# State-space layers: one PSUM tag for two rotating decay buffers, or one tag for each buffer

## Chip, cores and metric

The kernel runs on one core of a Trainium2 chip. The metric is the device time of one execution in microseconds (us), as the median of the runs. Beside it there is one execution recorded by the hardware profiler, from which all views of the profile come.

## What is computed

The network has four layers on x of shape 8 x 384 x 32 x 32, each `x = x + layer(group_norm(x))`. Layers 0 and 2 are Mamba state-space layers over 1,024 tokens per sample, with 768 inner channels and 16 states (layer 2 adds a layer norm and an MLP). Layer 1 is a deformable convolution, layer 3 a shift of channels with a small blur. The part that matters here is the recurrence of layers 0 and 2, for each channel d and state n:

```python
def step(h, inp):
    dt_t, B_t, C_t, u_t = inp
    dA = jnp.exp(dt_t[..., None] * A)
    h = dA * h + (dt_t * u_t)[..., None] * B_t[:, None, :]
    y = jnp.einsum('bdn,bn->bd', h, C_t)
    return (h, y)
...
y = jnp.swapaxes(ys, 0, 1) + u * D
y = y * jax.nn.silu(z)
return y @ out_proj_w.T
```

## The kernel before

`Net.ssm_layer` (called for layer 0 and, with the MLP and the shift part, for layer 2) cuts each sample into two halves of 512 tokens. A half is a *step*; there are 16 of them in a layer, and two that belong to one sample are called a pair here (h = 0, then h = 1). A step holds 6 blocks j of 128 channels, and for each block 8 pairs m of states. One (step, j, m) is a *unit*: 48 in a step, 768 in a layer. A unit works on tiles of 128 partitions x 2 states x 512 tokens in fp32:

- `decays` (L434 to L438): ACT computes exp(dt * A) for the two states, one ACTIVATE each, into the tile `da`. This tile lies in PSUM and takes two of the eight banks.
- `inputs` (L440 to L443): POOL computes `db` = dt * u * B in SBUF (three buffers).
- `scan` (L445 to L454): DVE runs the recurrence as one `tensor_tensor_scan` over da and db. It writes h over da in PSUM. For some units ("mine" in the code: m = 0 and 4 in layer 0, m = 0 in layer 2) it writes h to the SBUF tile `hs` instead.
- `keep_last` (L456 to L459): in the steps with h = 0, ACT copies the last state of each row to `st`; the second half starts from it.
- `with_c` (L461 to L467): the product of h and C into `hs`, on DVE (L467), or for the "mine" units on POOL (L464). In layer 2, POOL adds the two states of five of the eight m (`add_pair`, L471).
- `read_out` (L474 to L486): PE sums hs over the states with identity matmuls into the PSUM tile `y` (L484; in layer 0 the D term enters by L480).

When a block's eight units are read out, `close` (L500 to L504) lets DVE multiply y by the gate and write it to u; `out_proj` (L511 to L517) uses u in the next step. The work of the next and previous steps (group norm, input projection `inner`, gate projection `z_proj`, softplus of dt `soft_*`, output projection, MLP) is spread between the units by `plan`. It gives each piece a unit of the step at which it is put behind that unit's own work on ACT, DVE, POOL or PE.

The order of instructions on each engine is thus written out by hand (`manual_schedule`). In the loop over units, iteration i issues in this order: ACT's planned pieces (`run(act[t])`), scan(i), with_c(i) if it is DVE's, keep_last(i), decays(i + 2), DVE's planned pieces, inputs(i + 3), with_c(i) if it is POOL's, POOL's and PE's planned pieces. So decays run two units ahead of their scan, inputs three. Close of block j - 1 is a planned piece of DVE at unit m = 1 of block j.

PSUM's eight banks hold three one-bank tiles of the pool `mm`, two two-bank tiles of the pool `dap`, and `y`. Before the change both tiles of `dap` have one tag, "da", with two buffers. Which of the two buffers a tile gets is decided when the program is built, in the builder's own estimate of which buffer comes free when. In the finished program it is fixed: a tile's first write waits for the last use of the tile that held this buffer before. The same pool serves the shift part (`over_y`, L1706) with 24 tiles.

## Time and profile before

| | us |
|---|---|
| median of 3 runs (9463.35 to 9469.98) | 9464.09 |
| the profiled execution | 9470.15 |
| its span, first to last instruction | 9468.3 |
| layer 0, from the first to the last scan | 63.2 to 3008.5 |
| layer 2, from the first to the last scan | 5953.1 to 9182.3 |
| L438, decays on ACT: 3,072 instructions, mean | 0.691 |
| L453, scan on DVE: 1,536 instructions, into da / into hs, mean | 2.290 / 2.280 |
| L467, C product on DVE: 1,248, mean | 1.225 |
| L464, C product on POOL: 288, mean | 2.355 |
| L443, inputs on POOL: 1,536, mean | 2.354 |

A row of the groups of instructions gives line, engine, operation, tiles, count, busy time, mean duration in ns, and the idle time of the engine just before these instructions with what ended most of it. A row of the list of waits gives who waited for whom, the total in us, how many times, and the longest. A row of a timeline gives start and length in us, engine, line, operation, tiles and count; in brackets is the idle time of that engine ahead of it and what ended it. PEld is TensorE's weight load. A row of the table by windows gives the window, its length, busy time and count of PE, PEld, DVE, ACT and POOL, then the granted TensorE clock, the DMA share and GB/s.

### The profile page before, as it was taken

The numbers are of one execution on the slowest core, as the hardware profiler recorded it, in microseconds if no ns is written. First come the engines' busy times: TensorE is split into PE (matmuls) and PEld (weight loads), VectorE is DVE, ScalarE is ACT, GpSimd is POOL, SyncE is SP. The second block draws the span as 40 slices with busy tenths as digits, with TensorE's granted clock in tenths as the row PEclk, the third lists the DMA queues.
The fourth block names the chain that finished last, engine by engine and source line by source line (L and its number), as shares of the span: only waits on it lengthen the run. The fifth ranks groups of instructions, "written<-read, shape, count | busy, mean of one in ns | idle before, by whom it ended". The sixth has DMA issues, their size and how long they took to land. (4 is left out here: it accounts for less than half of the span.)

```text
span 9468.3 us, 87246 instructions
## 1 busy us (share of the span) xinstructions
PE 8498.2 (90%) x27916; PEld 4527.1 (48%) x27916; DVE 8092.7 (85%) x8857; ACT 6476.0 (68%) x10147; POOL 5825.0 (62%) x3825
## 2 busy tenths in 40 slices
PE   7888888889887999999999997699999999999987
PEld 3333333333333677777777776244343443434333
DVE  7989999999997678778778877899999999999973
ACT  6666666666664678778778777667777777777750
POOL 7989989898897000000000000899999999999974
PEclk8999999999998999999999998799999999999998
DMA  2111211121121333333333333233232433323436
GB/s 94 66 56 46 85 56 49 52 83 56 50 79 40 80 77 89 92 80 88 89 83 87 90 80 87 93 99 96 90 95 88 126 107 96 92 91 90 123 99 127
DMA packets 566064, 791.97 MB, mean 84 GB/s; under 512 B 244243, under 2 KB 397235, under 8 KB 542041
## 3 DMA queue, kind: packets, MB, share of 16 engines
q1 hardware_dynamic: 503492, 775.85, 28.2%
q10 hardware_dynamic: 62100, 10.44, 0.7%
q8 instruction: 223, 3.65, 0.2%
q14 instruction: 249, 2.03, 0.1%
HBM read 716.49 MB, written 69.66 MB: 83 GB/s over the span
## 5 line engine op out<-in xcount | busy, mean ns | idle before, releaser
L443 POOL TENSOR_TENSOR db<-du,bc 128x1024 f32<-128x1024 f32 x1536 | 3607.0, 2354 | 356.3 <-DVE hs L453 184.7
L453 DVE TENSOR_TENSOR_SCAN da<-da,db 128x1024 f32<-128x1024 f32 x1248 | 2857.4, 2290 | 220.5 <-ACT da L438 170.0
L484 PE MATMUL y<-hs,ident 128*128 128x512 f32 x5184 | 2602.9, 639 | 382.2 <-DVE hs L467 229.8
L438 ACT ACTIVATE da<-dt,na 128x512 f32<-128x512 f32 x3072 | 2119.4, 691 | 917.0 <-DVE hs L467 653.8
L411 POOL TENSOR_TENSOR dt<-dt,sp_e 128x512 f32<-128x512 f32 x192 | 243.9, 1270 | 2929.1 <-DVE sp_e L403 2929.1
L484 PEld LDWEIGHTS y<-hs,ident 128*128 128x128 f32 x5184 | 1020.4, 203 | 1860.6 <-issue 1115.9
L1516 PE MATMUL wacc<-fsm,fxk 128*128 128x221 f32 (+34 forms) x10624 | 1667.7, 316 | 91.5 <-DVE fsm L1486 88.8
L1516 PEld LDWEIGHTS wacc<-fsm,fxk 128*128 128x128 f32 x10624 | 1580.6, 196 | 228.4 <-DVE fsm L1486 151.7
L467 DVE TENSOR_TENSOR hs<-da,bc 128x1024 f32<-128x1024 f32 x1248 | 1528.5, 1225 | 91.7 <-DVE da L453 2.3
L1486 DVE TENSOR_TENSOR fsm<-fhy,fhx 128x170 f32<-128x170 f32 (+42 forms) x3216 | 1171.5, 431 | 342.5 <-PE wacc L1516 315.6
L1446 ACT ACTIVATE fhy<-fpyx,cell 128x416 f32<-128x416 f32 (+9 forms) x1280 | 645.6, 576 | 386.8 <-DVE fsm L1486 386.8
L1469 DVE TENSOR_TENSOR fxk<-fxt,fwk 128x1024 f32<-128x1024 f32 (+1 forms) x688 | 788.2, 1182 | 10.8 <-ACT fxt L1248 10.8
L464 POOL TENSOR_TENSOR hs<-hs,bc 128x1024 f32<-128x1024 f32 x288 | 678.3, 2355 | 41.7 <-ACT st L459 41.6
L453 DVE TENSOR_TENSOR_SCAN hs<-da,db 128x1024 f32<-128x1024 f32 x288 | 656.8, 2280 | 49.0 <-POOL db L431 36.1
L471 POOL TENSOR_TENSOR hs<-hs 128x512 f32<-128x512 f32 x480 | 608.9, 1268 | 4.0 <-DVE hs L467 3.5
L567 PE MATMUL ps_m<-hid,wm 128*128 128x512 f32 x1152 | 536.8, 611 | 30.2 <-ACT hid L560 25.3
L545 PE MATMUL ps_h<-t,wm 128*128 128x512 f32 x1152 | 535.9, 603 | 16.5 <-DVE x L574 16.3
L1451 ACT ACTIVATE fhy<-fhy,cols 128x1344 f32<-128x1344 f32 (+10 forms) x368 | 530.8, 1442 | 12.0
L459 ACT COPY st<-da 128x2 f32<-128x2 f32 x624 | 97.8, 157 | 504.3 <-DVE hs L467 503.0
L1157 PE MATMUL ps_off<-fxn,fow 128*98 128x465 f32 (+10 forms) x896 | 386.6, 579 | 0.0
L1433 ACT ACTIVATE fhx<-fpyx,cell 128x544 f32<-128x544 f32 (+8 forms) x640 | 379.9, 666 | 0.0
L567 PEld LDWEIGHTS ps_m<-hid,wm 128*128 128x128 f32 x1152 | 221.6, 195 | 330.8 <-issue 262.4
(203 smaller groups left out, 9865.4 us busy)
## 6 DMA issues: line engine op xcount, KB each, us to landing
bc<-bcd SPq DMA_DIRECT2D x256, 1024.0 KB
fpyx<-fposd SPq DMA_DIRECT2D x640, 256.0 KB
wm<-in_w SPq DMA_DIRECT2D x96, 768.0 KB
x<-x SPq DMA_DIRECT2D x71, 768.0 KB
winr<-in_win SPq DMA_DIRECT2D x192, 192.0 KB
x<-in_x SPq DMA_DIRECT2D x40, 768.0 KB
fpyx<-fposd SPq DMA_DIRECT2D x24, 1024.0 KB
wm<-in_wout SPq DMA_DIRECT2D x48, 384.0 KB
```

The source lines that it names most:

```text
L438: nc.scalar.activation(da[:, i, :], s["dt", j], AF.Exp, scale=na[:, j, n : n + 1])
L443: nc.gpsimd.tensor_tensor(db, du, s["bc"][m][:, 0], ALU.mult)
L453: nc.vector.tensor_tensor_scan(h1, da1, db1, 0.0, ALU.mult, ALU.add)
L464: nc.gpsimd.tensor_tensor(s["hs", m], s["hs", m], c, ALU.mult)
L467: nc.vector.tensor_tensor(hs, s["da", m], c, ALU.mult)
L471: nc.gpsimd.tensor_tensor(hs[:, 0, :], hs[:, 0, :], hs[:, 1, :], ALU.add)
L484: nc.tensor.matmul(s["y"], self.ident, s["hs", m][:, i, :], start=first and i == 0, stop=k == NU - 1 and i == n - 1,)
L567: nc.tensor.matmul(ps, s["w2"][:, f, o * P : (o + 1) * P], s["hid", q][:, f, :], start=(f == 0), stop=(f == 3))
L1446: nc.scalar.activation(hy[:, at : at + (yb - ya) * W], pyx[:, 0, ya * W : yb * W], AF.Abs, bias=bias)
L1469: nc.vector.tensor_tensor(t[:, :n], x, wk[:, j : j + 1, :].to_broadcast([P, n, P]), ALU.mult)
L1486: nc.vector.tensor_tensor(self.sub(sm, at, [(r * w, n), (w, r), (1, w)]), self.sub(hy, hy_at[by] + xa, [(r * W, n), (W, r), (1, w)]), self ...
L1516: nc.tensor.matmul(a[:, ya - 4 * o : yb - 4 * o, xa:xb], k, self.sub(sm, sm_at[by], [(w, yb - ya), (1, w)]), start=False, stop=False,)
```

## The change

The pool gets one buffer per tag, and the tiles get two tags, chosen by the parity of m (units) or of c (chunks of the shift part). As 8 units make a block, parity alternates from unit to unit throughout. The two buffers have the same size and banks as before; a tile of unit k always gets the buffer of unit k - 2.

```diff
@@ ssm_layer
-            dap = ctx.enter_context(tc.tile_pool(name=f"da{li}", bufs=2, space=PSUM))
+            dap = ctx.enter_context(tc.tile_pool(name=f"da{li}", bufs=1, space=PSUM))
@@ decays
-                da = s["da", m] = dap.tile([P, 2, TS], F32, name="da", tag="da")
+                da = s["da", m] = dap.tile([P, 2, TS], F32, name="da", tag=f"da{m % 2}")
@@ over_y (shift part)
-            ps = d["psy", c] = dap.tile([P, 2, TS], F32, name="ps_y", tag="da").rearrange("p a b -> p (a b)")[:, :CH]
+            ps = d["psy", c] = dap.tile([P, 2, TS], F32, name="ps_y", tag=f"da{c % 2}").rearrange("p a b -> p (a b)")[:, :CH]
```

## The prediction

> **What bounds the kernel now.** I read the page first, for the engines' shares and the 40 slices.

> ```profile
> PE 8498.2 (90%) x27916; PEld 4527.1 (48%) x27916; DVE 8092.7 (85%) x8857; ACT 6476.0 (68%) x10147; POOL 5825.0 (62%) x3825
> DVE  7989999999997678778778877899999999999973
> POOL 7989989898897000000000000899999999999974
> ```

> No engine leads by itself. In the two state-space layers (slices 1 to 13 and 26 to 38) DVE and POOL are both near nine tenths. So I then took the busy time of two stretches, one pair of steps (96 units) of layer 0 and one of layer 2.

> ```profile
> 437.80:809.80 372.00, 326.75 (x709) 136.21 (x708) 340.38 (x235) 240.58 (x408) 333.65 (x211) 0.93 0.17 61
> 6776.00:7182.00 406.00, 383.58 (x877) 161.79 (x876) 378.74 (x282) 295.52 (x468) 379.44 (x259) 0.98 0.33 100
> ```

> The columns are length, then PE, PEld, DVE, ACT, POOL busy. DVE is idle 31.6 us of 372 and 27.3 of 406, POOL 38.4 and 26.6. The limit is therefore a chain that passes between DVE, PE and POOL, and what DVE waits for decides. The list of waits has two rows on the decays:

> ```profile
> ACT da L438 <- DVE hs L453: 194.5, 140, 3.1
> DVE da L453 <- ACT da L438: 170.0, 161, 2.2
> ```

> ACT's decays wait for a scan that writes hs (a unit whose C product is POOL's), and then DVE's next scan waits for the decays. One such place, first in ACT's timeline, then in DVE's:

> ```profile
> 520.27 0.15 ACT L459 COPY st<-da 128x2 f32<-128x2 f32 x1
> 521.90 1.42 ACT L438 ACTIVATE da<-dt,na 128x512 f32<-128x512 f32 x2 [1.48 <-DVE hs L453]
> ```

> ```profile
> 518.45 1.23 DVE L467 TENSOR_TENSOR hs<-da,bc 128x1024 f32<-128x1024 f32 x1
> 519.59 2.28 DVE L453 TENSOR_TENSOR_SCAN hs<-da,db 128x1024 f32<-128x1024 f32 x1
> 521.79 0.66 DVE L403 SCALAR_TENSOR_TENSOR sp_e<-sp_w,ps_dt 128x512 f32<-128x512 f32 x1
> 523.41 2.30 DVE L453 TENSOR_TENSOR_SCAN da<-da,db 128x1024 f32<-128x1024 f32 x1 [0.96 <-ACT da L438]
> ```

> The decays of 521.90 are those of the scan of 523.41 (unit k). They could have been written from 520.42 on: the tile of unit k-2 was free when its C product (518.45) ended at 519.68. They wait until 521.87, when the scan of unit k-1 has ended, because in this program their tile lies in the bank pair of unit k-1. DVE then idles 0.96 us.

> [...] gaps of 0.96 us recur here, though the space is there and only the choice of buffer is bad. [...] So decays moved beside a scan should slow neither. The trace agrees: 802 scans with over 1 us of decays beside them take 2.290 us on average, 280 with none 2.282; a decay takes 0.691 us elsewhere and 0.693 at these places, where DVE mostly idles.

> **The change part by part.** (1) *What it moves.* In the built programs every engine has the same instructions in the same order. Before, 110 of 1,560 tiles of the pool lie in the banks of the tile just before (70 in layer 0, 40 in layer 2, none in the shift part); after, none. Only waits differ. At each of the 110 places the decays of unit k lose the wait for scan k-1. The wait moves to the instruction behind them: 94 times to the copy of the last state (L459, which reads that scan's output), 16 times to the decays of k+1.

> (2) *What DVE idles there.* Read scan by scan at those 110: 23 places of 1.54 us (layer 0, m = 5), 47 of 0.96 (layer 0, m = 1; one is 1.31), 40 of 0.96 to 1.62 in layer 2. Sum 127.8 us.

> (3) *How much ACT lets go.* The decays cannot start before ACT's preceding instruction ends. So a place gives the smaller of DVE's gap and ACT's idle time before the decays. At m = 1 in layer 0 ACT idles mostly 1.2 to 1.6, so the whole 0.96 goes. At m = 5 it idles 0.67 (a gate with two table loads is just ahead), so 0.65 of 1.54 goes; 1.27 and 1.24 in the block j = 1. At 14 of the layer 2 places ACT is late by itself: nothing. Sum: layer 0 63.5 us (6.1, 8.5, 8.3, 8.3, 7.9, 8.1, 8.1, 8.2 by pair of steps), layer 2 24.5 (4.36 in the first pair, 2.88 in seven). Together 88.0.

> (4) *What PE takes back.* From 455.7 to 511.8 PE runs out_proj, z_proj, inner and read-outs without a wait:

> ```profile
> 457.53 2.74 PE L517 MATMUL ps_o<-u,wout 128*128 128x512 f32 x6
> ...
> 511.81 0.70 PE L484 MATMUL y<-hs,ident 128*128 128x512 f32 x1 [1.18 <-DVE hs L467]
> ```

> and inside it DVE's close already waits for PE:

> ```profile
> 494.17 0.69 DVE L504 TENSOR_TENSOR u<-y,sz 128x512 f32<-128x512 f32 x1 [0.33 <-PE y L484]
> ```

> Three places lie between (459.39, 474.87, 490.28): what DVE wins there it waits at 494.17. In seven pairs this costs 7 x 0.96 + 8.7 (m = 5) + 5.9 (the third place) = 21.3 us. The first pair has no output projection of an earlier step, so it keeps all. At the other places read closely, y is ready 3.0 to 6.2 us before the close, and PE next waits for DVE (559.6, 588.9, 617.8, 628.5 for the group norm's mean), so its later full stretch starts earlier by as much. Layer 0 keeps 63.5 - 21.3 = 42.2.

> (5) *What POOL takes back.* In the first pair of layer 2 POOL runs without a wait for DVE from 6094 to 6187, and DVE waits 3.34 us for it at 6184.98; the two places in it (0.52 + 0.96) are lost. Elsewhere POOL waits for scans right at the places or soon after, and until it does, db is ready at least 1.8 us before its scan in the cases read: more than one place moves the scan. Layer 2 keeps 23.0.

> (6) *What ACT gives in addition.* After a place ACT is 1.42 us early, DVE 0.96. In layer 2 two short DVE waits that ACT ends follow (6835.01: 0.35; 6901.91: 0.14). I take both in seven pairs: 3.4. Their ends are 0 and 3.4.

> (7) *The new waits.* Behind the copy or the decays of k+1 are queued ACT's further work and POOL's C product (which waits for that copy). The wait ends with scan k-1, and there the old program only began the decays of k; all of it is earlier by up to 1.42 us. Cost 0. From both sides: at worst ACT stands for the scan's 2.28 less the decays' 1.42, 0.86 us, in which it stood idle before too; at best the 1.42 of (6). PE, SP and DMA get no other order: 0.

> Sum: 42.2 + 23.0 + 3.4 = 68.6 us. The profiled execution, 9470.15 (span 9468.3 and 1.9 around it), becomes 9401.5. It is 6.1 over the median of 9464.09; the same saving from there gives 9395.5.

> **The rivals.** *PE takes nothing back* (for: DVE waits at that close are short, 0.33 to 1.32; against: PE has no gap there): 88.0 + 3.4 = 91.4, so 9372.7. *All gaps close* (against: ACT's table loads): 127.8, so 9336.3. *PE takes layer 0 whole*: the full PE stretch of each second step, 628.5 to 705, where DVE waits 3.3, 3.1, 1.0 and 2.1 us for PE, starts by something that does not move. For it: its first weight load also waits for ACT, 4.2 us. Against: the matmul itself starts 2.7 later, on DVE's gn_mv. Then layer 2 alone counts, 26.4: 9437.7. *POOL is the bound* (93% in layer 2; against: it waits for scans right at the places): within 10 us, 9460. *Slower: the granted PE clock falls.* [...] the clock is 0.93 in layer 0, 0.98 in layer 2. PE sets the pace for some 56 + 76 us per pair in layer 0 and about 80 in layer 2 (6898.9 to 6937.7 and a like one), eight times: 1.7 ms. It decides from a fall of 4% there; at 6% it costs 102, net +33: 9497. Against: layer 2 is busier on PE and has the higher clock.

> **How the numbers follow.** Forecast 0.58; PE takes nothing back 0.14; all gaps 0.03; layer 0 lost (wholly, or half with some 48 us left) 0.15; POOL 0.06; slower 0.04. The likeliest time is 9395.5. The range goes from 9372 (nothing taken back) to 9438 (layer 0 lost) and holds 0.87; leaving out either end would leave too much. A difference under 0.2% (19 us) can't be told from none: faster 0.90, same 0.06, slower 0.04.

> **What would show it.** The row of ACT's decays waiting for the scan of hs should fall from 194.5 to near nothing, and DVE's wait for the decays from 170.0 to 60 to 85 (the rest at m = 5 and in layer 2). The scan row's gap at 523.41 should vanish. DVE's wait for PE y at L504 should grow from 33 us by about 20. A pair of layer 0 should take 5.2 us less, a pair of layer 2 3.4. A close that waits no longer than before would show (4) wrong; a pair of layer 0 unchanged, the keeping; scans or decays longer by over 1%, the overlap.

## The result and the profile after

| | before | after | difference |
|---|---|---|---|
| median of the runs, us | 9467.03 (9463.35 to 9472.97) | 9389.55 (9387.00 to 9393.83) | -77.5 |
| ratio, 95% interval | | 0.9919 [0.9907, 0.9931] | |
| profiled execution, us | 9470.15 | 9393.83 | -76.3 |
| up to the first scan of layer 0 | 63.2 | 64.3 | +1.2 |
| layer 0, first to last scan | 2945.4 | 2908.9 | -36.4 |
| between the layers' scans (layer 1) | 2944.6 | 2944.3 | -0.2 |
| layer 2, first to last scan | 3229.1 | 3191.0 | -38.1 |
| after the last scan | 286.1 | 283.4 | -2.7 |

The change is faster by 0.8%, 9 us more than forecast and inside the range. The parts do not fit as well as the sum: layer 0 was to give 42.2 us and gave 36.4, layer 2 was to give 26.4 (steps 5 and 6) and gave 38.1. That these two errors have opposite signs and partly cancel is luck. The stretch after the last scan takes 279.7 to 286.4 us from kernel to kernel, whatever was edited; I do not attribute its 2.7.

The page of the kernel after, the lines of before's first fence:

```profile
PE 8473.1 (90%) x27891; PEld 4507.2 (48%) x27916; DVE 8088.9 (86%) x8857; ACT 6489.3 (69%) x10147; POOL 5825.4 (62%) x3825
...
DVE  7999999999996678778778777899999999999973
...
POOL 7989999999896000000000000899999999999974
```

DVE, ACT and POOL are busy for nearly as long as before, within 0.3% (DVE 8088.9 us against 8092.7, ACT 6489.3 against 6476.0); only idle time went. The same pair of steps in each layer, by windows:

```profile
425.86:792.33 366.47, 325.91 (x712) 135.99 (x711) 340.31 (x236) 241.29 (x409) 333.63 (x211) 0.93 0.18 62
6710.00:7111.55 401.55, 385.06 (x874) 163.08 (x874) 378.48 (x283) 294.90 (x466) 379.62 (x259) 0.97 0.33 101
```

The pair of layer 0 is 5.5 us shorter than before's 372.00, the one of layer 2 4.5 shorter than 406.00 (before's two windows start 10 and 21 us later in their pairs; from first scan to first scan its pairs take 372.04 and 406.19). DVE's and POOL's busy times are those of before. The waits on the decays, and the close's wait for PE:

```profile
ACT da L438 <- DVE hs L453: 74.8, 55, 3.1
...
DVE da L453 <- ACT da L438: 64.1, 69, 2.2
...
DVE u L504 <- PE y L484: 48.0, 21, 3.5
```

DVE's wait for the decays fell from 170.0 to 64.1 us, into the forecast 60 to 85. The close's wait grew from 33.3 to 48.0. ACT's row fell from 194.5 to 74.8 and not to near nothing. I had not split that row: sorted by the scan that ends each wait, 126.4 us of before's were waits for scan k-1 (96 of the 110 places), and 68.1 were units m = 2 and 6 of layer 0, which wait for scan k-2, the owner of their buffer in strict turn too. All 55 waits that remain are of that second kind (47 in layer 0, 8 in layer 2).

The place shown before (scan of 523.41), now in ACT's timeline:

```profile
518.20 0.15 ACT L459 COPY st<-da 128x2 f32<-128x2 f32 x1
518.39 1.42 ACT L438 ACTIVATE da<-dt,na 128x512 f32<-128x512 f32 x2
519.83 0.19 ACT L459 COPY st<-hs 128x2 f32<-128x2 f32 x1
519.93 1.41 ACT L438 ACTIVATE da<-dt,na 128x512 f32<-128x512 f32 x2
```

and in DVE's:

```profile
516.38 1.23 DVE L467 TENSOR_TENSOR hs<-da,bc 128x1024 f32<-128x1024 f32 x1
517.51 2.28 DVE L453 TENSOR_TENSOR_SCAN hs<-da,db 128x1024 f32<-128x1024 f32 x1
519.71 0.66 DVE L403 SCALAR_TENSOR_TENSOR sp_e<-sp_w,ps_dt 128x512 f32<-128x512 f32 x1
520.29 2.29 DVE L453 TENSOR_TENSOR_SCAN da<-da,db 128x1024 f32<-128x1024 f32 x1
```

The decays of 518.39 are written during the scan of 517.51, with no idle time ahead of them. The copy of the last state (519.83) now stands behind them and starts when that scan ends. The scan of 520.29 follows L403 without a gap. It even starts 0.08 us before L403's end (519.71 + 0.66), so a closed place gives 1.04 us, not the 0.96 of the gap.

In what follows, *the ledger* is how much earlier (+) each scan starts than before, unit by unit of a pair (0 to 47 the first step, 48 to 95 the second). It shows where time is won, and where it is given back.

### The profile page after: what moved, and what is told of

Read it like the earlier page. It is cut to its first block, busy times and chain, and to the rows that moved or that the text cites. A ratio compares the mean times of both kernels' runs of the same rounds, so it can differ in the third digit from the quotient of the medians.

```text
span 9392.0 us, 87221 instructions
## 1 busy us (share of the span) xinstructions
PE 8473.1 (90%) x27891; PEld 4507.2 (48%) x27916; DVE 8088.9 (86%) x8857; ACT 6489.3 (69%) x10147; POOL 5825.4 (62%) x3825
## 5 line engine op out<-in xcount | busy, mean ns | idle before, releaser
L453 DVE TENSOR_TENSOR_SCAN da<-da,db 128x1024 f32<-128x1024 f32 x1248 | 2857.4, 2290 | 125.1 <-ACT da L438 64.1
L484 PE MATMUL y<-hs,ident 128*128 128x512 f32 x5184 | 2598.4, 637 | 377.5 <-DVE hs L467 216.9
L438 ACT ACTIVATE da<-dt,na 128x512 f32<-128x512 f32 x3072 | 2120.8, 691 | 812.2 <-DVE hs L467 665.2
L484 PEld LDWEIGHTS y<-hs,ident 128*128 128x128 f32 x5184 | 1013.1, 202 | 1853.0 <-issue 1094.2
L467 DVE TENSOR_TENSOR hs<-da,bc 128x1024 f32<-128x1024 f32 x1248 | 1528.5, 1225 | 91.6 <-DVE da L453 1.4
L453 DVE TENSOR_TENSOR_SCAN hs<-da,db 128x1024 f32<-128x1024 f32 x288 | 656.9, 2281 | 52.0 <-POOL db L431 35.8
L464 POOL TENSOR_TENSOR hs<-hs,bc 128x1024 f32<-128x1024 f32 x288 | 678.7, 2356 | 32.7 <-ACT st L459 32.3
L545 PE MATMUL ps_h<-t,wm 128*128 128x512 f32 x1152 | 538.5, 605 | 16.8 <-DVE x L574 16.6
L567 PE MATMUL ps_m<-hid,wm 128*128 128x512 f32 x1152 | 525.3, 600 | 20.1 <-ACT hid L560 17.2
L459 ACT COPY st<-da 128x2 f32<-128x2 f32 x624 | 98.2, 157 | 512.0 <-DVE hs L467 509.8
L567 PEld LDWEIGHTS ps_m<-hid,wm 128*128 128x128 f32 x1152 | 217.3, 192 | 314.8 <-issue 252.5
```

Source lines behind the costliest of these rows:

```text
L438: nc.scalar.activation(da[:, i, :], s["dt", j], AF.Exp, scale=na[:, j, n : n + 1])
L453: nc.vector.tensor_tensor_scan(h1, da1, db1, 0.0, ALU.mult, ALU.add)
L464: nc.gpsimd.tensor_tensor(s["hs", m], s["hs", m], c, ALU.mult)
L467: nc.vector.tensor_tensor(hs, s["da", m], c, ALU.mult)
L484: nc.tensor.matmul(s["y"], self.ident, s["hs", m][:, i, :], start=first and i == 0, stop=k == NU - 1 and i == n - 1,)
L545: nc.tensor.matmul(ps, s["w1"][:, k, f * P : (f + 1) * P], s["t"][:, k, :], start=(k == 0), stop=(k == G - 1))
```

## The experiments

Most kernels below write the choice of buffers out by hand: a table of units (of a pair) that take the buffer of the unit just before, and the tag from it. A unit that takes the buffer of the unit just before is called a *repeat*; where the two buffers alternate, the turns are *strict*. With exactly before's 110 repeats the built program is the program before, instruction for instruction.

```diff
+AGAIN = {0: ((5, 1, 8), (9, 1, 8), (13, 0, 8), (17, 0, 8), (25, 0, 8), (33, 0, 8), (37, 0, 8), (41, 0, 8), (49, 0, 8)), 2: ((9, 1, 8), (17, 0, 8), (25, 0, 1), (33, 0, 8), (41, 0, 8), (49, 0, 8))}
+side = lambda li, k: (k + sum(96 * p + u <= k for u, a, z in AGAIN[li] for p in range(a, z))) % 2
-            dap = ctx.enter_context(tc.tile_pool(name=f"da{li}", bufs=2, space=PSUM))
+            dap = ctx.enter_context(tc.tile_pool(name=f"da{li}", bufs=1, space=PSUM))
-                da = s["da", m] = dap.tile([P, 2, TS], F32, name="da", tag="da")
+                da = s["da", m] = dap.tile([P, 2, TS], F32, name="da", tag=f"da{side(li, 96 * s['b'] + 48 * s['h'] + 8 * j + m)}")
```

An entry (9, 1, 8) is unit 9 of the pairs 1 to 7. The diffs below show only what an experiment does to this table, or beside it. Ratios are to the kernel before, with their 95% intervals.

**More repeats.** Is a repeat the cause of a gap wherever it stands? The kernel before, with 56 more in layer 0.

```diff
-(49, 0, 8)), 2:
+(49, 0, 8), (57, 0, 8), (61, 0, 8), (65, 0, 8), (73, 0, 8), (81, 0, 8), (85, 0, 8), (89, 0, 8)), 2:
```

> The kernel before, with its 110 places and 56 more put in: in the second step of each pair of layer 0, units 57, 61, 65, 73, 81, 85 and 89 of the pair also take the banks of the unit just before. Theory (a place costs DVE its gap, unless a wait of DVE for PE follows that PE's own unbroken run sets): units 57, 61 and 65 lie ahead of such waits and cost nothing; 73, 81, 85, 89 cost 1.0 to 1.5 us each, so 32 to 45 us in 8 pairs: ratio to before 1.0034 to 1.0048. Rival (every place costs its gap, wherever it lies): 56 to 84 us, ratio 1.006 to 1.009. Second rival (banks don't matter as waits, the gain has another source): no change.

Measured: 9481.32, ratio 1.0015 [1.0008, 1.0021], +12.8 us. Two of the new places in DVE's timeline of this kernel:

```profile
651.89 2.30 DVE L453 TENSOR_TENSOR_SCAN da<-da,db 128x1024 f32<-128x1024 f32 x1 [0.96 <-ACT da L438]
...
667.30 2.30 DVE L453 TENSOR_TENSOR_SCAN da<-da,db 128x1024 f32<-128x1024 f32 x1 [1.54 <-ACT da L438]
```

At six of the seven units the gaps appear where I put them, in all pairs, and in the two main sizes of the 110 (0.96 and 1.54; at unit 85 the gap grew from 0.52). At unit 65 DVE waited 0.67 us for ACT already, and in seven pairs still does. So the cause is shown. Their price was missed, by more than half. By the ledger, units 57 and 61 lose 1.04 and 1.62 a pair and the next units have as much back in the sum of the pairs (unit 58 unevenly, from -0.6 to 3.4; it also swings between executions, see below). At unit 88 the new lateness dissolves a wait of 1.64 us for POOL's db. DVE's waits for PE at L504 and L537 fell in layer 0 from 31.2 and 28.5 us to 19.4 and 15.1. The second step of a layer 0 pair has slack in POOL and PE that pays for most of what a gap costs.

**Strict turns at the three places before the close only** (units 9, 13 and 17 of layer 0, 23 places). This is the disputed step 4.

```diff
-(9, 1, 8), (13, 0, 8), (17, 0, 8), (25, 0, 8)
+(25, 0, 8)
```

> The kernel before, with strict turns only at units 9, 13 and 17 of each pair of layer 0 (23 places); the other 87 stay. Theory (PE takes these back at the close of block 1): 0 to 3 us less than before, ratio 0.9997 to 1.000. Rival (they count in full): 23 x about 1.1, 25 us less, ratio 0.9973.

Measured: 9468.97, ratio 1.0001 [0.9992, 1.0009]. Nothing is won, as step 4 says. DVE's timeline of this kernel:

```profile
488.59 2.30 DVE L453 TENSOR_TENSOR_SCAN da<-da,db 128x1024 f32<-128x1024 f32 x1 [0.86 <-ACT da L438]
...
494.07 0.69 DVE L504 TENSOR_TENSOR u<-y,sz 128x512 f32<-128x512 f32 x1 [1.92 <-PE y L484]
```

The scan of 488.59 is before's of 490.28, 1.7 us earlier. The close starts at 494.07 against 494.17, and the pair itself began 0.11 earlier, so nothing is left: the close's wait for PE is now 1.92 instead of 0.33.

**Strict turns everywhere but there.** The complement: only those 23 repeats remain.

```diff
+AGAIN = {0: ((9, 1, 8), (13, 0, 8), (17, 0, 8)), 2: ()}
```

> Strict turns everywhere except at units 9, 13 and 17 of each pair of layer 0 (23 places as before). Theory: nearly all of the gain stays, 74 to 78 us less than before, ratio 0.9918 to 0.9922. Rival (the three count in full): 52 us less, ratio 0.9945.

Measured: 9388.74, ratio 0.9918 [0.9904, 0.9931], -79.8 us. All of the gain is there without the three places.

**Strict turns in layer 2 only**, to weigh the two layers.

```diff
-(41, 0, 8), (49, 0, 8)), 2: ((9, 1, 8), (17, 0, 8), (25, 0, 1), (33, 0, 8), (41, 0, 8), (49, 0, 8))}
+(41, 0, 8), (49, 0, 8)), 2: ()}
```

> Strict turns in layer 2 (and the shift part) alone; layer 0 keeps its 70 places. By the two traces layer 2 gave 38 us and the part after it 2.6: 38 to 41 us less than before, ratio 0.9957 to 0.9960. By the prediction's own working: 26 us less, ratio 0.9972.

Measured: 9434.99, ratio 0.9964 [0.9950, 0.9977], -33.6 us; in its trace layer 2 takes 3190.1 us (-39.0) and layer 0 2945.9 (as before). The interval of the ratio would still hold 26; the traces would not. Layer 2 takes 3228.8 to 3229.2 us in the three with before's repeats there (before and the two experiments above that leave it alone), and 3187.7 to 3194.6 in the six with strict turns. So layer 2 does give more than the forecast 26.4.

**The changed kernel again**, the same program in another execution.

> The changed kernel itself, once more, beside the next runs on the same chip: ratio to before 0.991 to 0.993.

Measured: 9397.42, ratio 0.9924 [0.9911, 0.9938], -71.1 us. Its trace has the layers at 2901.8 (-43.6) and 3194.4 (-34.7), where the first trace of the same program had -36.4 and -38.1. Why two executions of one program differ by 7 us in layer 0 is taken up below.

**Six unused matmuls ahead of the down-projection** (L567), in each step that has one: the kernel before, and PE is kept busy there. It adds work whose output nothing reads.

```diff
+            warm = lambda s: [nc.tensor.matmul(ps, mean_w, s["t"][:, 0, :], start=k == 0, stop=k == 5) for ps in [self.psum("warm")] for k in range(6)]
-                    ups = ((7, 8, 11, 13), (22, 23, 28, 29), (37, 38, 39, 40))
+                    put(pe, 33, warm, prev); ups = ((7, 8, 11, 13), (22, 23, 28, 29), (37, 38, 39, 40))
```

> The kernel before (all 110 places kept), with six matmuls of 512 columns added to TensorE's order in layer 2, into a PSUM tile that nobody reads, just ahead of the MLP's second down-projection (unit 33 of each step that has one). They compute nothing that is used. Theory (the extra gain of layer 2 at unit 41 comes from TensorE's clock: before, the down-projection starts after 2.1 to 2.8 us of idleness, and its first eight matmuls take 5.40 us; after, 3.70): with the gap filled they take about 3.7 us, and DVE's gap at unit 41 falls from 1.62 to the 0.96 of the false wait, in seven pairs: 3 to 6 us less than before, ratio 0.9994 to 0.9997. Rival (the extra gain comes from ACT's earlier start alone): the gap at unit 41 stays 1.62, and the added work costs 0 to 10 us.

Measured: 9501.66, ratio 1.0035 [1.0021, 1.0048], +33 us. I overfilled the hole. In its trace each of these fp32 matmuls is two records (L579: 24 in the two steps of a pair, 10.6 us busy), so six are 5.3 us; in the first steps the down-projection began mostly 8.1 us after scan 33 instead of 5.65. Its eight records did take 3.6 us instead of 5.40, but that is less than the delay: 0.4 to 0.8 us a pair are lost at unit 41. Most of the loss lies elsewhere: the same six matmuls stand in the second steps too, where the ledger loses 28 us at units 85 to 90. This run settles nothing.

**Two unused matmuls instead**, and only in the first step of each pair of layer 2.

```diff
-for k in range(6)]
+for k in range(2)]
-                    put(pe, 33, warm, prev); ups
+                    put(pe, 33, warm, prev if s["h"] == 0 else None); ups
```

> As e6, but two added matmuls (1.7 us of PE) in place of six (5.2 us, which overfilled the gap), and only in the first step of each pair of layer 2, in seven pairs; nobody reads what they compute. Theory (TensorE's clock): the down-projection still starts 5.65 us after scan 33, its first eight records take 3.7 us in place of 5.40, and DVE's gap at unit 41 falls from 1.62 to 0.96: 4 to 5 us less than before in layer 2. Rival (ACT's earlier start): eight records faster or not, the gap at unit 41 stays 1.62.

Measured: 9461.59, ratio 0.9994 [0.9985, 1.0003]; by the medians this can't be told from before. The trace tells it: layer 2 takes 3218.4 us (-10.7), and in all seven pairs the ledger wins 0.66 at unit 41, 0.33 at 42 and 0.70 at 44, 1.7 us in all, with useless work added (I had expected the 0.66 alone). DVE's gap at unit 41 is 0.96 in all seven, in place of 1.62:

```profile
6924.46 2.30 DVE L453 TENSOR_TENSOR_SCAN da<-da,db 128x1024 f32<-128x1024 f32 x1 [0.96 <-ACT da L438]
```

So the rival is out.

**Strict turns at unit 41 of layer 2 only.** If the repeat there were what costs time, this would win it.

```diff
-(33, 0, 8), (41, 0, 8), (49, 0, 8))}
+(33, 0, 8), (49, 0, 8))}
```

> The kernel before with strict turns only at unit 41 of each pair of layer 2 (8 places). The prediction gave such a place nothing, as ACT is late there by itself. Theory (ACT is late because PE is, and PE starts late and cold on account of unit 33): still nothing in seven pairs, 0 to 0.5 us in the first; the gap at unit 41 stays 1.5 to 1.62. Rival (a place counts by its own gap): 1.57 in each of seven pairs, 11 us less.

Measured: 9468.62, ratio 1.0002 [0.9993, 1.0011]; the gap at unit 41 stays (1.75 us in seven pairs). Nothing is won, as expected. The down-projection behind unit 33 is as slow as before in all seven:

```profile
6897.63 5.40 PE L567 MATMUL ps_m<-hid,wm 128*128 128x512 f32 x8 [2.78 <-ACT hid L560]
```

**Strict turns at unit 33 of layer 2 only** (its label says the opposite: all repeats but that of unit 33 are kept).

```diff
-(25, 0, 1), (33, 0, 8), (41, 0, 8)
+(25, 0, 1), (41, 0, 8)
```

> The kernel before with strict turns in layer 2 only at unit 33 of each pair (8 places). Theory: 1.17 in seven pairs at units 33 to 35, and as the down-projection behind it then starts with PE warm (its first eight records 3.7 us), the gap at unit 41 falls from 1.62 to the 0.96 of the false wait, which is still there: 1.17 + 0.65 in each pair, 12 to 14 us less than before in layer 2. Rival (the clock plays no part): 1.17 each, 8 to 9 us, and a gap of 1.62 at unit 41.

Measured: 9441.7, ratio 0.9971 [0.9960, 0.9983], -26.0 us. The ledger wins 1.04 at unit 33, 0.14 at 35, then 0.66, 0.33 and 0.70 at 41, 42 and 44: 2.9 a pair. I had not counted the last two. So 1.7 of these 2.9 us are won eight to eleven units after the place that was edited, at and behind a place whose repeat is still there. PE's run behind unit 33:

```profile
6892.94 3.70 PE L567 MATMUL ps_m<-hid,wm 128*128 128x512 f32 x8 [0.88 <-ACT hid L560]
```

The trace's layer 2 is 27.5 us shorter, of which seven times 2.9 and the first pair's 1.04 make 21; the rest moves at units 1, 9 and 55 to 57, differently in each pair.

**The input projection one unit later.** The changed kernel, and the first `inner` of layer 0 moved from unit 15 to 16, so that PE gets to the close's read-out sooner.

```diff
-                for d, t in enumerate((15, 16, 17, 24, 25, 26)):
+                for d, t in enumerate((15 if mlp else 16, 16, 17, 24, 25, 26)):
```

> The changed kernel with one input projection of layer 0 (6 matmuls, 2.6 us of PE) moved from unit 15 to unit 16 of each step, behind the last read-outs of block 1. Theory (PE's unbroken run ahead of block 1's close takes the three places back): DVE's waits at that close, 2.4 to 3.1 us in seven pairs, shrink by 2 to 2.5 us: 14 to 18 us less than the changed kernel, ratio to before 0.9899 to 0.9904. Rival (the close waits for something that this does not move): as the changed kernel, 0.992.

Measured: 9375.17, ratio 0.9900 [0.9885, 0.9915], -93 us (the changed kernel, timed beside it: -71). The list of waits of this kernel:

```profile
DVE u L504 <- PE y L484: 16.0, 8, 3.3
```

48.0 became 16.0 us. In the first steps, what is won there is lost again to DVE's other waits for PE and ACT. In the second steps, at the close ahead of unit 66, 2.06 us a pair are kept. So the ratio lies in the forecast range, but only the second steps bear the theory out.

**That, and two gates earlier.** The m = 5 gaps (16.6 us are left of before's 35.4) stand behind a gate on ACT; this moves the gates of blocks 0 and 4 of layer 0 one unit ahead.

```diff
-                    put(pe, (0, 9, 18, 27, 33, 41)[j], z_proj, s, j)
-                    g = (3, 11, 20, 29, 35, 44)[j]
+                    put(pe, (0, 9, 18, 27, 33 if mlp else 32, 41)[j], z_proj, s, j)
+                    g = ((3, 11, 20, 29, 35, 44) if mlp else (2, 11, 20, 29, 34, 44))[j]
```

> As e7, and the gates of blocks 0 and 4 of layer 0 one unit earlier on ACT (with the projection of block 4 one unit earlier on PE), so that their two table loads no longer stand just ahead of the decays at m = 5. Theory (the rest of the gap at m = 5, 0.9 us in 15 places, is ACT's table loads): 11 to 14 us less than e7, ratio to before 0.9885 to 0.989. Rival (ACT stays late, or the gate then waits for PE): as e7.

Measured: 9366.26, ratio 0.9893 [0.9878, 0.9908], -102 us, the shortest time here, though its interval overlaps that of the run before. It is 8.9 us less than that run, where 11 to 14 were expected. The m = 5 gaps fell to 3.0 us, and against that run the ledger wins 0.98 at units 5 and 37, 15.7 us in all; 2.0 to 2.2 are given back at unit 14 in four pairs and 0.5 at unit 48 in all.

## Why the prediction was right, and where it was wrong

**Steps 1 and 2, right.** DVE's gaps at the 110 places fell from 127.8 us to 33.7 (16.6 at m = 5 and 6.2 at m = 1 in layer 0, 10.9 in layer 2), and more repeats made more gaps.

**Step 3, right in layer 0.** The ledger shows 1.04 at each of the units 25, 33, 41 and 49, and 0.63 to 0.64 at 5 and 37, where ACT's gate limits it to the forecast 0.65. With those of the first pair (0.64 and 1.04 at 13 and 17) they sum to 44.5 us; the forecast 42.2 had 0.96 in place of 1.04.

**Step 4, right in what it costs and on which engine.** Units 9 and 13 win 1.04 and 1.23 and units 16 to 18 lose as much in the pairs 1 to 4; in pairs 5 to 7 0.6 to 0.8 is kept. The two experiments on these places gave 0 and all the rest. DVE's timeline of the changed kernel at this close:

```profile
485.06 0.69 DVE L403 SCALAR_TENSOR_TENSOR sp_e<-sp_w,ps_dt 128x512 f32<-128x512 f32 x1 [0.77 <-ACT st L459]
486.61 2.30 DVE L453 TENSOR_TENSOR_SCAN da<-da,db 128x1024 f32<-128x1024 f32 x1 [0.86 <-ACT da L438]
488.94 1.22 DVE L467 TENSOR_TENSOR hs<-da,bc 128x1024 f32<-128x1024 f32 x1
492.09 0.69 DVE L504 TENSOR_TENSOR u<-y,sz 128x512 f32<-128x512 f32 x1 [1.92 <-PE y L484]
```

The close waits 1.92 us, not 0.33. It also shows what I had not: at the third place DVE wins nothing even before the close, since ACT is late there (0.77 and 0.86). ACT in turn waits for PE's projection of dt:

```profile
482.45 0.69 ACT L396 ACTIVATE dt<-ps_dt,vec 128x512 f32<-128x512 f32 x1 [2.69 <-PE ps_dt L390]
```

Before, this wait was 0.30 us in this pair; over the seven pairs 0.3 to 1.3 became 2.6 to 3.6. So it is still PE that takes the three places back, but not at the close alone. In layer 0 the close's wait grew by 14.2 us (31.2 to 45.4), not by 20. Only 7.7 of the 14.2 are at the close meant here (0.33 to 1.32 us became 1.92 in each of seven pairs); 6.5 are at unit 58 and belong to what follows. In the second execution the wait is 39.0, 7.8 more than before.

**Why layer 0 gave 36.4.** In the first trace of the changed kernel 10 us are lost at the units 56 to 58. There DVE waits for PE's second-step run, from the group norm's matmul (gn_ps, L140) to the first output projection (L517). That run has another length in every execution, and it takes these us:

| run, pairs 0 to 6, us | 0 | 1 | 2 | 3 | 4 | 5 | 6 | sum |
|---|---|---|---|---|---|---|---|---|
| before | 19.54 | 22.20 | 19.56 | 18.91 | 21.88 | 21.79 | 21.77 | 145.7 |
| after | 23.29 | 22.04 | 23.29 | 21.97 | 18.92 | 21.98 | 23.25 | 154.7 |
| after, again | 19.56 | 21.80 | 22.20 | 21.91 | 18.92 | 21.96 | 19.39 | 145.7 |

The first and third executions differ by nothing in the sum, and layer 0 then gave 43.6 us, 1.4 from the forecast. The kernel with strict turns everywhere but at the three places has a sum of 145.8, and its layer 0 gave 42.1. The granted clock differs with the length. In pair 0, PE's timeline of the changed kernel, then of the same program again:

```profile
253.77 3.97 PE L140 MATMUL gn_ps<-gn_mv,gmat 128*128 128x2 f32 x18 [4.41 <-DVE gn_mv L132]
...
277.06 2.74 PE L517 MATMUL ps_o<-u,wout 128*128 128x512 f32 x6
```

```profile
252.66 3.97 PE L140 MATMUL gn_ps<-gn_mv,gmat 128*128 128x2 f32 x18 [4.42 <-DVE gn_mv L132]
...
272.21 2.74 PE L517 MATMUL ps_o<-u,wout 128*128 128x512 f32 x6
```

and the windows over these runs (the granted clock is the third number from the end), in the same order:

```profile
254.00:262.00 8.00, 8.00 (x23) 5.25 (x24) 7.90 (x7) 3.26 (x7) 7.11 (x6) 0.50 0.00 0
262.00:270.00 8.00, 8.00 (x24) 5.16 (x23) 7.21 (x6) 6.44 (x14) 6.79 (x8) 0.50 0.01 3
```

```profile
254.00:262.00 8.00, 8.00 (x23) 4.60 (x23) 7.90 (x8) 3.25 (x7) 7.19 (x5) 0.57 0.00 0
262.00:270.00 8.00, 8.00 (x27) 4.33 (x27) 7.97 (x6) 7.68 (x16) 7.63 (x8) 0.79 0.01 3
```

**Step 3 failed in layer 2, at unit 41.** "At 14 of the layer 2 places ACT is late by itself: nothing." Seven of these are unit 41 of the first steps. The ledger wins 1.57 there and 0.13 at 42: 1.7 us in each of seven pairs, 11.9 us in all, priced at zero. ACT is late there because it waits for PE (its input is ps_h), and PE's run begins with the down-projection, L567. I took the length of that run as given. PE's timeline of before, then of after:

```profile
6893.42 2.74 PE L493 MATMUL ps_z<-xn,winr 128*128 128x512 f32 x6
6898.94 5.40 PE L567 MATMUL ps_m<-hid,wm 128*128 128x512 f32 x8 [2.78 <-ACT hid L560]
```

```profile
6847.38 2.74 PE L493 MATMUL ps_z<-xn,winr 128*128 128x512 f32 x6
6851.01 3.70 PE L567 MATMUL ps_m<-hid,wm 128*128 128x512 f32 x8 [0.89 <-ACT hid L560]
```

In all seven pairs of before, PE idles 2.06 to 2.78 us ahead of these eight records (four matmuls) and they take 5.40 us. In all seven of after it idles 0.89 to 1.37, and they take 3.70. The clock in windows of 3 us from their start on, before and after:

```profile
6899.00:6902.00 3.00, 3.00 (x5) 1.38 (x6) 2.83 (x3) 2.89 (x6) 2.46 (x2) 0.63 0.02 5
6902.00:6905.00 3.00, 3.00 (x6) 1.14 (x6) 2.97 (x2) 2.94 (x4) 3.00 (x3) 0.80 0.00 0
```

```profile
6851.00:6854.00 3.00, 2.99 (x7) 1.44 (x8) 2.97 (x2) 2.80 (x4) 3.00 (x3) 1.00 0.25 71
6854.00:6857.00 3.00, 3.00 (x8) 1.33 (x7) 2.96 (x3) 2.69 (x4) 3.00 (x2) 1.00 0.00 0
```

The same stretch of before, cut at points of the 3.413 us grid:

```profile
6896.38:6899.79 3.41, 0.85 (x2) 0.49 (x3) 3.38 (x4) 3.38 (x3) 3.41 (x3) 1.00 0.19 58
6899.79:6903.20 3.41, 3.41 (x5) 1.33 (x4) 3.23 (x3) 3.27 (x7) 2.87 (x3) 0.50 0.02 5
6903.21:6906.62 3.41, 3.41 (x9) 1.52 (x8) 3.38 (x3) 3.36 (x4) 3.33 (x3) 1.00 0.00 0
```

PE is busy for 0.85 us of the first of these windows, and the clock of the next is 0.50, though PE has been running again for 0.85 us when it begins.

The strict turn at unit 33 brings that scan 1.04 us forward and L567 1.2 us (it starts 5.65 us after the scan of unit 33 before, mostly 5.52 after, 5.28 in the pair shown); PE idles less, its clock stays at 1.00, and the eight records end 1.7 us sooner beyond that. Where the run starts on the grid is no rival here: over all traces, with starts 2.6 to 2.9 us after its last point, the runs behind 1.35 to 1.36 us of idle time stay at clock 1.00 and those behind 2.06 to 2.79 do not. DVE's scan of unit 41 before, and after:

```profile
6925.79 2.30 DVE L453 TENSOR_TENSOR_SCAN da<-da,db 128x1024 f32<-128x1024 f32 x1 [1.62 <-ACT da L438]
```

```profile
6875.70 0.66 DVE L403 SCALAR_TENSOR_TENSOR sp_e<-sp_w,ps_dt 128x512 f32<-128x512 f32 x1
6876.30 2.30 DVE L453 TENSOR_TENSOR_SCAN da<-da,db 128x1024 f32<-128x1024 f32 x1
```

The rival for this step was that the repeat at unit 41 was the cost. It falls: strict turns there alone win nothing. The explanation by the clock holds: two unused matmuls in the idle time win the same 1.7 us with every repeat in place. PE's timeline of that kernel:

```profile
6895.33 1.88 PE L579 MATMUL warm<-t,mean_w 128*128 128x512 f32 x4
...
6898.28 3.70 PE L567 MATMUL ps_m<-hid,wm 128*128 128x512 f32 x8 [1.06 <-ACT hid L560]
```

The clock is 1.00 in both windows of 3 us from 6898 on, where before's from 6899 on have 0.63 and 0.80. 5.40 - 3.70 = 1.70, which is what its ledger wins per pair.

**Steps 5 and 6, right in size, step 5 not in the engine.** In the first pair of layer 2 the gain of unit 41 (+0.41, then -0.77) and half of that at 49 (-0.56) are given back; 3.0 us are kept of the pair's 4.36, about what step 5 left. But it is PE that takes them in this trace, at the closes ahead of units 42 and 50, which had no such waits before:

```profile
6082.18 0.76 DVE L503 SCALAR_TENSOR_TENSOR y<-u,vec,y 128x512 f32<-128x512 f32 x1 [0.67 <-PE y L484]
...
6113.52 0.76 DVE L503 SCALAR_TENSOR_TENSOR y<-u,vec,y 128x512 f32<-128x512 f32 x1 [0.48 <-PE y L484]
```

POOL's wait that step 5 named is 3.4 us, against 3.3 before. The two small waits of step 6 gave 0.38 and 0.13 us at units 19 and 35, forecast 0.35 and 0.14. Step 3's 2.88 and these 0.49 with the 1.70 and three times 0.08 make 5.3 a pair in seven pairs, 40 us with the first; layer 2 kept 38.1 and in the second execution 34.7. The rest goes at units 1, 9 and 55 to 58, by amounts that differ between the two executions of one program. I did not follow them further.

**Step 7, right.** The waits for the copy did not grow: those of POOL's C product fell from 41.6 us to 32.3, those of the scans stayed at 30.8. Scans into da take 2.290 us on average and decays 0.691, as before. More directly: the scans of unit k-1 at the 110 places had no decays beside them before and on average 1.00 us of them after, and took 2.281 us both times; the decays there took 0.693 and 0.692. So writing decays beside a scan, in the other bank pair, slowed neither here.

Of the rivals, "PE takes nothing back" (9372.7) and "PE takes layer 0 whole" (9437.7) fall with the experiments on the three places and the -36 to -44 us of layer 0; "all gaps close" (9336.3) falls with the 33.7 us of gaps that stay. The feared lower PE clock did not come: the mean is 0.951 against 0.947.

## What to carry to other kernels

When a pool rotates its buffers by the builder's estimate, read from the built program which tile really follows which: a tile placed in the buffer just used ties its producer to the unit just before, and two tags in turn cost no space here (the two buffers have the size and banks that they had). Price a gap by what is late next, place by place, and do not count those that lie ahead of a wait for another engine. And when a change moves the start of a TensorE run, read the run's granted clock and length again: here a start 1.2 us earlier went with a clock of 1.00 in place of 0.68 and eight records in 3.70 us in place of 5.40, which is more than the shift.

## What the hardware showed that I had not expected

- In 28 of 28 places, in the four kernels that leave unit 33 as before and fill nothing, the down-projection was slow behind 2.06 to 2.79 us of idle time (eight records 5.38 to 5.40 us, one stretch of 3.41 us at clock 0.50); behind 0.34 to 1.37 us it was not (3.70 us, clock 1.00). All 28 began 2.2 to 3.4 us after the last point of the grid; earlier starts after so long an idle time were not seen.
- Useless work won time: four records of 1.88 us in all shortened the run behind them by 1.70 us.
- One program's group norm runs have two lengths, 3.0 to 3.9 us apart, behind the same idle time, sorted without exception by where on the 3.413 us grid of the clock's changes they start; over a layer this moved the sum by 9 us between two executions.
